# Cross-attention with layer norm on one core: scores of one of four column groups of heads with 128 rows at a time instead of 64

## The chip, the cores and the metric

The kernel runs on one core of a Trainium2 chip. The metric is the device time of one execution in microseconds, median of several executions. An execution profiled by the hardware gives the trace, from which every span and wait below is taken. Engines go by the profile's names: PE is TensorE (PEld its weight loads), DVE is VectorE, ACT is ScalarE, POOL is GpSimd, SP is the engine that issues most transfers.

## The reference

Queries come from `x` (4 batches of 2048 rows, 512 wide), keys and values from a context of 77 rows per batch; 16 heads of 32. After the attention comes the output product, the residual and a layer norm.

```python
qs = (q @ wq).reshape(Bq, Lq, H, HD).transpose(0, 2, 1, 3)
ks_ = (k @ wk).reshape(Bq, Lk, H, HD).transpose(0, 2, 1, 3)
vs = (v @ wv).reshape(Bq, Lk, H, HD).transpose(0, 2, 1, 3)
scores = jnp.einsum('bhqd,bhkd->bhqk', qs, ks_) / jnp.sqrt(jnp.float32(HD))
scores = jnp.where(mask[:, None, :, :], -jnp.inf, scores)
attn_w = jax.nn.softmax(scores, axis=-1)
attn = jnp.einsum('bhqk,bhkd->bhqd', attn_w, vs)
attn = attn.transpose(0, 2, 1, 3).reshape(Bq, Lq, H * HD)
out = attn @ wo + q
mu = jnp.mean(out, axis=-1, keepdims=True)
var = jnp.mean((out - mu) ** 2, axis=-1, keepdims=True)
return (out - mu) / jnp.sqrt(var + EPS) * gamma + beta
```

## The kernel before

**Tiles.** The 8192 rows are 64 tiles of 128 rows. Query projections are made for groups of 512 rows (4 tiles); the product of weights and values goes by pairs of tiles, 256 rows. Products with the 512x512 weights split each operand into a high and a low part and add three products (high by high, high by low, low by high), in 4 steps of the contraction: 12 matmuls with 512 columns for one visit.

**TensorE's work by kind.** Four kinds make up nearly all of it, and each has its letter in the order table:
- Q, line 290 (`q_rows`): one of four 128-column blocks of the query projection of a group of 512 rows, tile `pq`, 12 matmuls, in the shape 128x128 (rows by columns of the array that the weights fill).
- S, line 414 (`scores`): the scores of one tile, in four banks `sc`. Head group `g` (0 to 3) and member `j` (0 to 3) give 16 heads. Heads of one `g` lie on the four 32-row strips of one 128-column block of the projection, so four products with 32 rows of contraction stand side by side in the array. The queries are the weights here; the 77 keys stream. `SR` = 64 splits the tile's 128 query rows into two halves: 4 groups times 2 halves times 4 members are 32 products in the shape 32x64. They are float32, and each is two passes in the profile, two weight loads and two matmul records.
- V, line 507 (`av`): attention weights times values for a pair of tiles, tile `pa`, 16 products in the shape 96x32.
- O, line 579 (`o_proj`): the output product of a tile, `po`, 12 matmuls in the shape 128x128.

**The other engines, per tile.** VectorE takes the scores with the mask and finds the row maxima (line 431, 16 calls), transposes (482), makes the low part of the attention output (540), copies projections (304), adds the residual (588). ScalarE makes the exponentials (446, 16 calls) and some casts; GpSimd normalises (461), splits `x` (273) and applies the affine part (621, 622). Transfers regroup the transposed weights `B` into `PT` (493).

**The order.** The tile framework schedules nothing here. The string `ORDER` lists every step, one word for each: `S36` is the scores of tile 36, `Q38` the third block of group 9, `V15` the values' product of pair 15. The words run in that order on every engine that they use, and semaphores keep the engines apart. Through the middle of the run TensorE's words repeat with a period of two tiles: S, V, S, Q, Q, O, O. Around the change in tile 36 they read S36, V15, S37, Q40, Q41, O31, O30. `SLOTS` names the buffer of every tile in the same order.

**NO_OPs.** `PADS` has one base-36 digit for each visit of kind Q (from the second group on) or O, in the order in which these stand in the program. `pad_steps` spreads that many NO_OPs (line 283, `idle`) over the 11 gaps between the visit's 12 matmuls. Before the change the middle of the run has 20 to 22 in each visit, two in nearly every gap.

Of the kernel before, what the change touches and what calls it, by code (L numbers as in the profile page):

```python
# [17 lines left out]
P = 128  # L18
# [3 lines left out]
NK = 77  # L22
# [11 lines left out]
for b in range(4):  # L34
# [6 lines left out]
SR = 64  # L41
# [128 lines left out]
}  # L170

PADS = (
    "f8680000000000000000000686000cddlmmllllllllmmmmmmmmmmmmmmmmmmmmikkkkkkkkkkkkkkkkkkkkkkkkkkkkkkjkkk00"
    "000000000000000000000000"
)


# [1 line left out]
def xattn_layernorm(  # L179
# [37 lines left out]
    def bank(name):  # L217
        return ps.tile([P, 512], F32, tag="mm" + next(slots["mm"]), name=name)
# [35 lines left out]
    def keys_of(h):  # L254
        return slice(TAIL_K, NK2) if h % 2 == 0 else slice(0, NK)
# [144 lines left out]
    def early_waits(mm, t):  # L400
        after = pe_words[pe_words.index(f"S{t}") + 1]
        for part in parts[int(after[1:])] if after[0] == "V" else ():
            info = mybir.DependencyInfo(mybir.DependencyClass.Sync, mybir.DependencyReason.DATA)
            tc.add_manual_dep(mm.ins, part.ins.name, info, reason="values' product waits ahead of the scores")

    def scores(t):
        qs, first = qd[t // 4], True
        rs = slice((t % 4) * P, (t % 4) * P + P)
        sc = scs[t] = [bank(f"sc_{t}_{j}") for j in range(GH)]
        for g in range(NG):  # L410
            for r0 in range(0, P, SR):
                for j in range(GH):
                    q = slice(HD * j, HD * (j + 1))
                    mm = nc.tensor.matmul(  # L414
                        sc[j][r0 : r0 + SR, g * NK : (g + 1) * NK],
                        qs[q, g, rs.start + r0 : rs.start + r0 + SR],
                        kct[q, g, t // TPB, keys_of(j)],
                        start=True,
                        stop=True,
                    )  # L420
                    if first:
                        early_waits(mm, t)
                    first = False
# [319 lines left out]
    for c in range(0, NC_D, 2):  # L743
# [14 lines left out]
        "i": lambda k, part: cast_xT(k // 2, k % 2 * 2), "j": lambda k, part: split_xT(k // 2, k % 2 * 2),  # L758
        "Q": lambda k, part: q_visit(*divmod(k, 4)), "q": lambda k, part: q_evac(*divmod(k, 4)),
        "S": lambda k, part: scores(k), "T": lambda k, part: maxima(k, q4 * part, q4 * part + q4),  # L760
        "e": lambda k, part: exps(k, q4 * part, q4 * part + q4), "r": lambda k, part: recip(k),
        "n": lambda k, part: normalise(k), "h": recip_half, "m": normalise_half, "t": lambda k, part: transp(k),
# [71 lines left out]
```

## Time and profile before

| what | before |
|---|---|
| median of 3 runs | 510.38 us (510.31 to 512.49) |
| the profiled execution | 509.93 us |
| its span, first to last instruction | 508.1 us |
| granted TensorE clock over the span | 0.998 |
| line 290 (Q), 12 matmuls of one kind each | x256, 395, 383 and 383 ns |
| line 579 (O) | x256, 399, 390 and 390 ns |
| line 507 (V) matmul records | x992, 382 ns |
| line 414 (S) weight loads | x4096, 130 ns |

A record of a matmul covers its whole way through the array, so records of neighbours overlap, and the pace is read from one start to the next. The counts of line 414 are twice those of the products, for the two passes. In rows of a timeline the columns are the start and the length in microseconds, then engine, line, operation, output and inputs, the shape (rows*columns of the array), the size of what streams, and the count.

### The profile page before, as it was taken

To read this page: it belongs to the slowest core of one execution; us is meant where nothing else is said; L and a number is where in the kernel's file an instruction comes from. 1 tells how busy PE (TensorE), PEld (TensorE's weight loads), DVE (VectorE), ACT (ScalarE), POOL (GpSimd) and SP (SyncE) were. 2 spreads that over 40 slices of the span, in tenths; PEclk is the share of its full clock that TensorE was granted. 3 is DMA by queue.
4 is the path that set the end of the run, shared out by engine and by line. 5 is a ranking of instruction groups with operands and counts; after the bars stand their busy time and mean duration, and the time that the engine had idled before them with its cause. 6 is when DMAs were issued, how large, how long until landed. Compare 5 with 4: busy or idle time off the path is not lost.

```text
span 508.1 us, 21810 instructions
## 1 busy us (share of the span) xinstructions
PE 497.6 (98%) x6834; PEld 384.0 (76%) x6834; DVE 471.3 (93%) x2565; ACT 465.6 (92%) x2228; POOL 420.0 (83%) x388
## 2 busy tenths in 40 slices
PE   8999999999999999999999999999999999999994
PEld 6987777777777777777777877777787777776663
DVE  5798999999999999999999999999999999999986
ACT  6699999998999999999999999999999999999622
POOL 2573756999978998989899898888989679999986
PEclk9999999999999999999999999999999999999999
DMA  8947767878987687796877678777777687777755
GB/s 298 397 154 215 177 185 171 239 195 237 261 239 220 192 243 198 204 261 189 237 205 239 198 218 229 213 226 211 225 207 219 182 225 214 209 210 198 213 153 228
DMA packets 59236, 110.96 MB, mean 218 GB/s; under 512 B 9430, under 2 KB 12270, under 8 KB 59126
## 3 DMA queue, kind: packets, MB, share of 16 engines
q1 hardware_dynamic: 54854, 101.63, 69.1%
q0 software_dynamic: 2624, 6.16, 4.4%
q10 hardware_dynamic: 1648, 1.77, 1.4%
q8 instruction: 60, 0.98, 0.9%
q14 instruction: 50, 0.41, 0.3%
HBM read 41.79 MB, written 16.78 MB: 115 GB/s over the span
## 4 chain that ended last, share of the span: by engine, by line
PE 85%; DVE 5%; DMA 4%; POOL 3%; SPq 2%; issue 1%; ACTq 0%; ACT 0%; DVEq 0%
PE pq L290 33%; PE po L579 28%; PE sc L414 10%; PE pa L507 10%; PE pv L341 2%; DVE pbuf L431 1%; DVE B L482 1%; PE pk L313 1%; DMA xtl<-x 1%; DMA PT<-B 1%; SPq L493 1%; DMA first_xth<-xw 1%; POOL mvt L646 1%; PE pq L724 1%; DVE q L304 0%
## 5 line engine op out<-in xcount | busy, mean ns | idle before, releaser
L446 ACT ACTIVATE pbuf<-pbuf,nm 128x77 f32<-128x77 f32 x1024 | 352.4, 350 | 3.6 <-DVE nm L431 3.4
L446 ACT ACTIVATION_READ_ACCUMULATOR pbuf<-pbuf,nm 128x1 f32 x1024 | 195.3, 191 | 0.0
L431 DVE CUSTOM_DVE_ANT_0 pbuf<-sc,mb 128x77 f32<-128x77 f32 x1024 | 170.8, 232 | 6.8 <-PE sc L414 3.6
L461 POOL TENSOR_TENSOR pbuf<-pbuf,ri 128x1232 f32<-128x1232 f32 x63 | 142.8, 2268 | 29.1 <-DVE ri L456 27.6
L579 PE MATMUL po<-woh,AH 128*128 128x512 f32 x256 | 102.1, 399 | 0.4 <-DVE nm L431 0.4
L290 PE MATMUL pq<-xth,wqh 128*128 128x512 f32 (+1 forms) x256 | 101.2, 395 | 0.3
L579 PE MATMUL po<-woh,AL 128*128 128x512 f32 x256 | 99.8, 390 | 0.8 <-DVE AL L540 0.8
L579 PE MATMUL po<-wol,AH 128*128 128x512 f32 x256 | 99.7, 390 | 0.0
L290 PE MATMUL pq<-xth,wql 128*128 128x512 f32 (+1 forms) x256 | 98.1, 383 | 0.0
L290 PE MATMUL pq<-xtl,wqh 128*128 128x512 f32 (+1 forms) x256 | 98.1, 383 | 0.0
L482 DVE STREAM_TRANSPOSE B<-pbuf 128x1280 f32<-128x1280 f32 x64 | 96.1, 1501 | 0.9 <-POOL pbuf L461 0.2
L431 DVE DVE_READ_ACCUMULATOR2_ANT nm<- 128x1 f32 x1024 | 83.8, 82 | 0.0
L273 POOL TENSOR_TENSOR xtl<-xtf,xth 128x1024 fp32r<-128x1024 f32 x28 | 67.3, 2406 | 4.3 <-ACT xth L269 4.3
L622 POOL TENSOR_TENSOR o<-o,bet 128x512 f32<-128x512 f32 x51 | 66.0, 1294 | 4.0
L414 PEld LDWEIGHTS sc<-kct,q 32*64 32x64 f32 x4096 | 51.2, 130 | 22.2 <-issue 11.0
L621 POOL TENSOR_TENSOR o<-o,gam 128x512 f32<-128x512 f32 x51 | 67.0, 1314 | 0.2 <-issue 0.2
L414 PE MATMUL sc<-kct,q 32*64 32x77 f32 x4096 | 60.6, 238 | 0.0
L507 PE MATMUL pa<-PT,vsb 96*32 96x256 f32 x992 | 59.7, 382 | 0.0
L579 PEld LDWEIGHTS po<-woh,AH 128*128 128x128 f32 x256 | 48.0, 188 | 13.9 <-issue 1.7
L290 PEld LDWEIGHTS pq<-xth,wqh 128*128 128x128 f32 x256 | 48.1, 188 | 12.3 <-issue 1.2
L579 PEld LDWEIGHTS po<-woh,AL 128*128 128x128 f32 x256 | 48.1, 188 | 11.6 <-DVE AL L540 1.5
L290 PEld LDWEIGHTS pq<-xth,wql 128*128 128x128 f32 x256 | 48.1, 188 | 9.7
(127 smaller groups left out, 641.9 us busy)
## 6 DMA issues: line engine op xcount, KB each, us to landing
PT<-B SPq DMA_DIRECT2D x337, 128.0 KB
xtf<-xT SPq DMA_DIRECT2D x28, 512.0 KB
o<-x SPq DMA_DIRECT2D x56, 256.0 KB
out<-o SPq DMA_DIRECT2D x56, 256.0 KB
PT<-B POOLq DMA_DIRECT2D x29, 128.0 KB, 3.9
stage_a<-wk SPq DMA_DIRECT2D x4, 256.0 KB
stage_b<-wo SPq DMA_DIRECT2D x4, 256.0 KB
stage_a<-xT SPq DMA_DIRECT2D x2, 512.0 KB
```

The lines of the kernel that those rows point to most:

```text
L273: nc.gpsimd.tensor_tensor(l[:, c : c + 2], fx.pop((g, c)), xh[g][:, c : c + 2].bitcast(F32), ALU.subtract)
L290: nc.tensor.matmul(pq, w[:, c, m * P : (m + 1) * P], r[g][:, c, rs], start=(n == 0), stop=(n == 11))
L341: nc.tensor.matmul(pv[: rows.stop - rows.start], ctx_s[c][i][:, rows], v[c], start=(n == 0), stop=(n == 11))
L414: mm = nc.tensor.matmul(sc[j][r0 : r0 + SR, g * NK : (g + 1) * NK], qs[q, g, rs.start + r0 : rs.start + r0 + SR], kct[q, g, t // TPB, keys ...
L431: nc.vector.tensor_tensor_reduce(pb[:, h // 2, (h % 2) * NK : (h % 2 + 1) * NK], scs[t][j][:, g * NK : (g + 1) * NK], mb[:, t % TPB, keys_ ...
L446: nc.scalar.activation(pb[:, h // 2, (h % 2) * NK : (h % 2 + 1) * NK], pb[:, h // 2, (h % 2) * NK : (h % 2 + 1) * NK], AF.Exp, bias=nmax[t ...
L461: nc.gpsimd.tensor_tensor(pv, pv, rv.to_broadcast((P, NP, 2, NK)), ALU.mult)
L482: nc.vector.transpose(bt.rearrange("p c q r -> p q c r"), pbuf[t % NPB].rearrange("p q (c r) -> p q c r", c=5),)
L507: nc.tensor.matmul(pas[b, g // 2][HD * j : HD * (j + 1), (g % 2) * BLK : (g % 2 + 1) * BLK], vsb[:, 2 * b // TPB, h % 2, HD * (h // 2) : H ...
L579: nc.tensor.matmul(pos[t], a[:, c, rs], w[:, c, :], start=(first and c == 0 and n == 0), stop=(c == NC_D - 1 and n == 2),)
L621: nc.gpsimd.tensor_tensor(o, o, gam, ALU.mult)
L622: nc.gpsimd.tensor_tensor(o, o, bet, ALU.add)
```

## The change

In `scores`, the group `g == 1` takes all 128 rows as weights at once, so that its products have the shape 32x128; the groups 0, 2 and 3 keep their two halves of 64. A tile then has 8 + 4 + 8 + 8 = 28 products. What each bank holds at the end is the same. `PADS` is another string: 1479 NO_OPs in the program instead of 1466, and another distribution. The order of the words, the buffers and the other engines' instructions stay as they were.

```diff
 PADS = (
-    "f8680000000000000000000686000cddlmmllllllllmmmmmmmmmmmmmmmmmmmmikkkkkkkkkkkkkkkkkkkkkkkkkkkkkkjkkk00"
-    "000000000000000000000000"
+    "f8682000000000000000000000000086cddddddb1hllll1dllmmmmmmmmmmmmmmmmmmmmmmmmmmmmmmmmmmmmmkkkkkkkkk4kkkk"
+    "mmmmm0000000000000000000"
 )
...
         for g in range(NG):
-            for r0 in range(0, P, SR):
+            rows = P if g == 1 else SR
+            for r0 in range(0, P, rows):
                 for j in range(GH):
                     q = slice(HD * j, HD * (j + 1))
                     mm = nc.tensor.matmul(
-                        sc[j][r0 : r0 + SR, g * NK : (g + 1) * NK],
-                        qs[q, g, rs.start + r0 : rs.start + r0 + SR],
+                        sc[j][r0 : r0 + rows, g * NK : (g + 1) * NK],
+                        qs[q, g, rs.start + r0 : rs.start + r0 + rows],
                         kct[q, g, t // TPB, keys_of(j)],
```

The first place is TensorE's order in the scores of tile 36. A row is a product: the bank it writes, the keys and queries it reads, and rows by columns of its result. Before, these eight rows are the second column group, its lower and its upper half:

```order
L414 MATMUL sc_36_0_5891<-kct_74,q_9_5475 64x77
L414 MATMUL sc_36_1_5892<-kct_74,q_9_5475 64x77
L414 MATMUL sc_36_2_5893<-kct_74,q_9_5475 64x77
L414 MATMUL sc_36_3_5894<-kct_74,q_9_5475 64x77
L414 MATMUL sc_36_0_5891<-kct_74,q_9_5475 64x77
L414 MATMUL sc_36_1_5892<-kct_74,q_9_5475 64x77
L414 MATMUL sc_36_2_5893<-kct_74,q_9_5475 64x77
L414 MATMUL sc_36_3_5894<-kct_74,q_9_5475 64x77
```

Now the last row of the first group, the four of the second, and the first of the third:

```order
L415 MATMUL sc_36_3_5588<-kct_74,q_9_5169 64x77
L415 MATMUL sc_36_0_5585<-kct_74,q_9_5169 128x77
L415 MATMUL sc_36_1_5586<-kct_74,q_9_5169 128x77
L415 MATMUL sc_36_2_5587<-kct_74,q_9_5169 128x77
L415 MATMUL sc_36_3_5588<-kct_74,q_9_5169 128x77
L415 MATMUL sc_36_0_5585<-kct_74,q_9_5169 64x77
```

Eight products have become four, and the shape changes once ahead of them and once behind.

The second place is TensorE's order in the visit Q30 (third block of group 7), as an example of the NO_OPs that moved. Before, the visit begins so:

```order
L290 MATMUL pq_7_2_4231<-xth_7_3371,wqh_70 128x512
L283 NO_OP x2
L290 MATMUL pq_7_2_4231<-xtl_7_3441,wqh_70 128x512
L283 NO_OP x2
L290 MATMUL pq_7_2_4231<-xth_7_3371,wql_71 128x512
```

And now:

```order
L290 MATMUL pq_7_2_3981<-xth_7_3190,wqh_70 128x512
L283 NO_OP
L290 MATMUL pq_7_2_3981<-xtl_7_3256,wqh_70 128x512
L290 MATMUL pq_7_2_3981<-xth_7_3190,wql_71 128x512
L290 MATMUL pq_7_2_3981<-xth_7_3190,wqh_70 128x512
```

Of 22 NO_OPs in this visit one is left. Elsewhere it goes the other way: the eight visits from Q56 to O48 had none and have 20 to 22.

More of the change, by code (lines that the diff above doesn't have):

```diff
@@ L172 @@
 PADS = (
-    "f8680000000000000000000686000cddlmmllllllllmmmmmmmmmmmmmmmmmmmmikkkkkkkkkkkkkkkkkkkkkkkkkkkkkkjkkk00"
-    "000000000000000000000000"
+    "f8682000000000000000000000000086cddddddb1hllll1dllmmmmmmmmmmmmmmmmmmmmmmmmmmmmmmmmmmmmkkkkkkkkk4kkkk"
+    "mmmmm0000000000000000000"
 )
```

## The prediction

> **What bounds the kernel now.** I read the page first: busy times, granted clock, chain.
>
> ```profile
> span 508.1 us, 21810 instructions
> PE 497.6 (98%) x6834; PEld 384.0 (76%) x6834; DVE 471.3 (93%) x2565; ACT 465.6 (92%) x2228; POOL 420.0 (83%) x388
> PEclk9999999999999999999999999999999999999999
> PE 85%; DVE 5%; DMA 4%; POOL 3%; SPq 2%; issue 1%; ACTq 0%; ACT 0%; DVEq 0%
> L414 PE MATMUL sc<-kct,q 32*64 32x77 f32 x4096 | 60.6, 238 | 0.0
> ```
>
> TensorE is busy all the time, at full clock, and the chain that ended last lies on it for 85%. Four engines are above 80%, though, so I asked next for the stretches between one pair of tiles and the next.
>
> ```profile
> core 0: us, PE busy (x) PEld busy (x) DVE busy (x) ACT busy (x) POOL busy (x), PEclk, DMA share, GB/s
> 264.93:279.68 14.75, 14.75 (x212) 11.46 (x209) 13.54 (x79) 14.40 (x71) 13.47 (x12) 1.00 0.76 225
> 279.68:294.43 14.75, 14.75 (x213) 11.46 (x209) 14.17 (x82) 14.35 (x70) 12.96 (x11) 1.00 0.72 207
> ```
>
> Two tiles take 14.75 us, all of it TensorE. ScalarE has 0.35 us to spare, VectorE 0.6 to 1.2. So a longer score product lengthens the loop at once, while a shorter one may save some 0.3 us a loop before ScalarE holds it. The chain of waits shows the loop's parts:
>
> ```profile
> 109.88 5.68 PE po L579 x24
> 277.00 0.88 PE sc L414 x55
> 277.89 1.86 PE pa L507 x32
> 279.75 0.88 PE sc L414 x53
> 280.63 5.68 PE pq L290 x24
> 286.31 5.44 PE po L579 x24
> ```
>
> A tile's scores take 0.88 us, 64 times. The first row is of two visits without a NO_OP, the last two of visits with 22 each: the visit right behind scores is 5.68 us with and without. NO_OPs are hidden behind matmuls of 0.23 us.
>
> **One tile's scores, record by record.** Each of the 32 products leaves two matmul records and two weight loads (4096 records over 64 tiles). The timeline of tile 36, in windows that end later and later, then its weight loads:
>
> ```profile
> 276.94 0.32 PE L414 MATMUL sc<-kct,q 32*64 32x77 f32 x8
> 276.94 0.39 PE L414 MATMUL sc<-kct,q 32*64 32x77 f32 x16
> 276.94 0.46 PE L414 MATMUL sc<-kct,q 32*64 32x77 f32 x24
> 276.94 0.52 PE L414 MATMUL sc<-kct,q 32*64 32x77 f32 x32
> 277.31 0.51 PE L414 MATMUL sc<-kct,q 32*64 32x77 f32 x27
> 276.94 0.95 PE L414 MATMUL sc<-kct,q 32*64 32x77 f32 x64
> 276.93 0.45 PEld L414 LDWEIGHTS sc<-kct,q 32*64 32x64 f32 x34 [0.35 <-issue]
> L414 PE MATMUL sc<-kct,q x4096: 224/225/277, 20.9 to 466.5; 32*64 32x77 f32 x196
> ```
>
> Eight records run side by side (four row groups of the array times two column halves), and a wave of eight costs 0.067 us (0.39 to 0.46 to 0.52). A record lasts 0.225, so the 32nd starts at 0.52 - 0.225 = 0.295. At the wave pace the 64th would start at 0.295 + 4 x 0.067 = 0.56; it starts at 0.95 - 0.225 = 0.725. So 0.16 us is lost, and the load row tells where: by 277.30 only 34 loads (17 products) have begun, and the next records begin at 277.31. The first 17 products are at hand at once; the other 15 then arrive one per 0.017 us or so ((277.66 - 0.12 - 277.31) / 14, with 0.12 for a product's two passes).
>
> **What a change of shape costs.** The places before and behind:
>
> ```profile
> 276.39 0.39 PE L579 MATMUL po<-wol,AH 128*128 128x512 f32 x1
> 276.62 0.39 PE L579 MATMUL po<-woh,AL 128*128 128x512 f32 x1
> 277.81 0.37 PEld L507 LDWEIGHTS pa<-PT,vsb 96*32 96x32 f32 x12
> 280.56 0.50 PE L290 MATMUL pq<-xth,wqh 128*128 128x512 f32 x1
> 280.90 0.39 PE L290 MATMUL pq<-xtl,wqh 128*128 128x512 f32 x1
> 281.12 0.40 PE L290 MATMUL pq<-xth,wql 128*128 128x512 f32 x1
> 280.67 0.19 PEld L290 LDWEIGHTS pq<-xtl,wqh 128*128 128x128 f32 x1
> ```
>
> Output matmuls follow each other at 0.23, but the scores begin 0.31 behind the last one (276.93 - 276.62): 0.09 more. The last score record starts at 277.66, the values' first load at 277.81: 0.15, where the next wave would have come within 0.067: again 0.09. No load of the new shape was pulled ahead: "[0.35 <-issue]" is a load engine that waits for nothing the profile shows. Then the first 128-column load lies bare: the second matmul comes 0.34 behind the first instead of 0.23, and the second load 0.11 behind the first (280.56, 280.67). So 128 columns load in 0.11 and 64 in about 0.055.
>
> **The change, part by part.** It removes 4 of 32 products a tile: 8 matmul records and 8 loads, 512 of each over the run. It adds two places where the shape changes, 32x64 to 32x128 and back. The trace of before has no change of the column half alone: each of its three kinds of boundary (128x128 or 96x32 against 32x64) changes rows and columns. Upper bound: it costs what these cost. Lower bound: nothing, loads pulled ahead as within the scores. I take the upper one, because all three kinds show the same 0.09 however different their columns are, and no row shows a boundary for less.
>
> Terms per tile, against a score product at the wave pace (0.88 - 0.16 = 0.72):
> - two boundaries. The next wave's first record normally starts 0.067 - 0.047 = 0.02 behind the last record of the one ahead (eight starts 0.0067 apart, estimated from (0.32 - 0.276)/7, with the 0.277 of the source row for the first ones); now 0.15: 2 x 0.13 = +0.26.
> - bare loads: +0.11 into the second group, +0.055 into the third.
> - inside the second group the second pass waits for its 128-column load, 0.11 instead of 0.067: +0.04.
> - four records a wave instead of eight: -0.03.
> - the 0.16 us of late products does not come back: the boundaries give the last 15 more time than they need.
>
> 0.72 + 0.26 + 0.165 + 0.04 - 0.03 = 1.155, so +0.275 per tile. By the skill's page this is what happens: the Trainium skill, TensorEngine Tiling (Array Packing), Key Properties, states that changing the tiling mode, not just the tile, drains TensorE. The three boundaries here agree with 0.09 each; whether it holds for columns alone no run here shows yet, and with no drain the sum would be the first rival's.
>
> The same skill speaks still harder against the change in TensorE: Matmul & The Clock Gate, "What overlaps and what doesn't": loads overlap matmuls in flight only if the row group differs. By that, each pass of the second group would be load plus stream, another 0.067 a tile, and the time 531. The trace disagrees: the load at 280.67 runs while the first matmul on the same rows streams until 280.90.
>
> How many tiles count? The late part of the chain and of the waits:
>
> ```profile
> 402.97 1.20 DVE AL L540 x2
> 415.67 1.42 DVE B L482
> 456.18 1.91 PE pa L507 x32
> 462.30 6.36 DMA xtl<-x
> PEld po L579 <- DVE nm L431: 0.5, 1, 0.5
> ```
>
> Around 402 to 417 VectorE leads and TensorE waits 0.5 us for it (the waits between 411 and 420); a later TensorE uses that up first. Past 458 the chain runs over transfers and VectorE, so the last tile's scores (465.73) do not count. 63 x 0.275 - 0.5 = +16.8. The profiled execution took 509.93 (1.8 around its span): 526.7. The median of the runs shown is 0.45 above it: 527.
>
> **NO_OPs** go from 1466 to 1479 and stand elsewhere (none before, 20 to 22 in eight late visits; 12 to 13 instead of 21 in several early ones). I cost them at nothing: the 5.68 against 5.68 above. They matter as a cover for instruction fetching:
>
> ```profile
> q8 instruction: 60, 0.98, 0.9%
> 203.24 0.96 PE sc L414 x52
> 262.20 0.93 PE sc L414 x55
> ```
>
> 60 packets of 16 KB fit TensorE's some 15,400 instructions, about 256 each (an estimate). Before, a loop's length is nearly a whole number of packets; 32 records fewer a loop shift that, and a late fetch could fall into scores. The worst scores in the loop, whatever their cause, are 0.05 to 0.08 longer than 0.88. The bound is that on every tile, 64 x 0.08 = 5 us; with boundaries inside the scores there is time to spare, so I take 0.
>
> **Rivals.**
> 1. Faster: a change of columns alone drains nothing. Then the 0.16 us pause is what counts. At the wave pace the scores are 0.72; the second group's two loads add 0.04 each, and the first of them starts 0.03 late because both halves must be free: 0.83, or -0.05; the queue allows at most 4 x 0.017 = -0.067. Tiles past 398 hardly count (VectorE leads), say 55 to 60: -2.7 to -4.0, so 506.4 to 507.7, about 507.3. For it: rows stay 32, and loads are pulled ahead freely within the scores. Against: every boundary seen.
> 2. Slower by less: no drain, but the 128-column load must wait until the passes before it have streamed. Rival 1 plus 0.067 on the way in and about 0.05 on the way out: +0.06 a tile, 63 x 0.06 = 3.8, 514. It decides from the point where a load cannot enter a half that still streams.
> 3. No change: rival 1's gain is eaten by ScalarE (0.35 us idle a loop, fully busy in places before 161) or by fetches of 0.05 in most scores: 510 +- 2.
>
> **Numbers.** Forecast (drain) 0.46, its own range 521 to 530; rival 1 0.30, rival 2 0.12, rival 3 0.12. 0.5%, 2.55 us, is about what a measurement of this kernel can tell from no change. Rival 1 is beyond it 4 times in 5: faster 0.24. Same: 0.06 of rival 1 and rival 3, 0.18. Slower: 0.58. The range reaches from rival 1's middle, 506.8, to 530: it leaves out the best of rival 1 and the worst of the drain.
>
> **What would show it.** Right: tile 36's scores at 1.1 to 1.2 us in the chain, gaps of 0.15 before and behind the 32*128 records, 15.3 us a pair, ScalarE idle above 0.8 us a loop. Rival 1: scores at 0.81 to 0.84 with 32*128 loads beginning within 0.03 of the last 32*64 record. Rival 2: about 0.94. I would be wrong in the term of the boundary if the gaps are there but shorter, and in the count of tiles if scores lengthen and the loop does not.

## The result, and the profile after

The changed kernel takes 526.72 us (median of 5 runs, 526.58 to 527.15). The kernel before took 510.59 us beside it (5 runs, 510.31 to 512.49). The ratio is 1.0307, with a 95% interval of 1.0288 to 1.0327: slower by 3%. The profiled execution took 526.61 us.

The page after, the lines that answer to those of before (span, busy times, granted clock, shares of the chain that ended last), and VectorE's reading of the scores:

```profile
span 524.7 us, 20798 instructions
PE 515.4 (98%) x6322; PEld 391.5 (75%) x6322; DVE 473.8 (90%) x2565; ACT 468.5 (89%) x2228; POOL 419.0 (80%) x388
PEclk9999999999999999999999999999999999999999
PE 94%; POOL 3%; DMA 1%; DVE 1%; issue 0%; SPq 0%; ACT 0%; DVEq 0%
L432 DVE CUSTOM_DVE_ANT_0 pbuf<-sc,mb 128x77 f32<-128x77 f32 x1024 | 171.1, 232 | 15.8 <-PE sc L415 12.7
```

TensorE runs 512 matmul records fewer (6322 for 6834) at the same clock and is busy 17.8 us longer. The other engines' busy time has hardly moved, and VectorE waits 12.7 us in all for the scores instead of 3.6 (the row of line 431 before). TensorE leads the chain for 94% of the span instead of 85%: where VectorE and transfers led near the end of before, TensorE does now.

The same stretches from pair to pair as before, busy time of each engine:

```profile
core 0: us, PE busy (x) PEld busy (x) DVE busy (x) ACT busy (x) POOL busy (x), PEclk, DMA share, GB/s
274.00:289.28 15.28, 15.28 (x197) 11.67 (x193) 13.58 (x79) 14.49 (x70) 13.14 (x11) 1.00 0.73 217
289.28:304.57 15.29, 15.29 (x196) 11.68 (x192) 14.14 (x80) 14.50 (x71) 13.30 (x11) 1.00 0.68 202
```

A pair takes 15.28 to 15.29 us instead of 14.75, all of it TensorE. The chain of waits in the loop shows which step grew:

```profile
286.32 1.16 PE sc L415 x56
287.48 1.86 PE pa L508 x32
289.35 1.16 PE sc L415 x56
290.51 5.67 PE pq L290 x24
296.18 5.44 PE po L580 x24
```

Scores went from 0.88 to 1.16 us; values, Q and O are as they were (1.86, 5.67, 5.44). Added up over the run, from each tile's first score record to the first record of the next step, the scores went from 57.4 to 74.3 us, +16.9. All other stretches of TensorE from the first visit of line 290 on together stayed at 425.8 (425.86 and 425.82). The span grew by 16.6, because that first visit begins 0.3 us earlier now (17.92 and 17.60). So the whole lengthening lies in the scores.

Inside tile 36, the timeline in windows that begin and end at different records (start, length, engine, line, operation, shape of the array, what streams, count):

```profile
286.25 0.39 PE L415 MATMUL sc<-kct,q 32*64 32x77 f32 x16
286.57 0.20 PEld L415 LDWEIGHTS sc<-kct,q 32*128 32x128 f32 x4
286.57 0.31 PEld L415 LDWEIGHTS sc<-kct,q 32*128 32x128 f32 x8
286.57 0.46 PE L415 MATMUL sc<-kct,q 32*128 32x77 f32 x8
286.96 0.37 PEld L415 LDWEIGHTS sc<-kct,q 32*64 32x64 f32 x32
287.14 0.34 PE L415 MATMUL sc<-kct,q 32*64 32x77 f32 x16
287.41 0.16 PEld L508 LDWEIGHTS pa<-PT,vsb 96*32 96x32 f32 x8
```

Read them as three changes of shape. The first group's last record ends at 286.25 + 0.39 = 286.64, and the first load of the wide group starts at 286.57. The wide group's last record ends at 286.57 + 0.46 = 287.03, the next narrow load starts at 286.96. The last narrow record ends at 287.14 + 0.34 = 287.48, the values' first load starts at 287.41. Each time the first load of the new shape starts 0.07 us ahead of the modelled end of the last record of the old one, and never earlier, though loads of the same shape are pulled far ahead. The boundaries of before show the same 0.07: the last score record there ends at 277.66 + 0.225, the values' first load starts at 277.81. From record start to load start this is 0.154 us on the way in, behind records of 0.225, and 0.199 on the way out, because the wide group's second-pass records last 0.270 (the 0.045 more is the whole difference). The wide loads of the second pass come 0.11 behind those of the first (0.31 - 0.20). The last 32 loads run through in 0.37 without a gap: the pause of before, between the 17th product and the 18th, is gone.

### The profile page after: what moved, and what is told of

Its sections match the earlier page's. It is cut to its first block, busy times and chain, and to the rows that moved or that the text cites. A ratio compares the mean times of both kernels' runs of the same rounds, so it can differ in the third digit from the quotient of the medians.

```text
span 524.7 us, 20798 instructions
## 1 busy us (share of the span) xinstructions
PE 515.4 (98%) x6322; PEld 391.5 (75%) x6322; DVE 473.8 (90%) x2565; ACT 468.5 (89%) x2228; POOL 419.0 (80%) x388
## 4 chain that ended last, share of the span: by engine, by line
PE 94%; POOL 3%; DMA 1%; DVE 1%; issue 0%; SPq 0%; ACT 0%; DVEq 0%
PE pq L290 33%; PE po L580 31%; PE sc L415 14%; PE pa L508 11%; PE pv L341 2%; PE pk L313 1%; PE pq L725 1%; DMA first_xtl<-xw 1%; POOL mvt L647 1%; PE po L567 1%; POOL PT L494 0%; DMA PT<-B 0%; DVE B L483 0%; POOL xth L623 0%; POOL xtl L622 0%; POOL xth L622 0%
## 5 line engine op out<-in xcount | busy, mean ns | idle before, releaser
L432 DVE CUSTOM_DVE_ANT_0 pbuf<-sc,mb 128x77 f32<-128x77 f32 x1024 | 171.1, 232 | 15.8 <-PE sc L415 12.7
L415 PEld LDWEIGHTS sc<-kct,q 32*64 32x64 f32 (+1 forms) x3584 | 58.6, 138 | 32.8 <-issue 11.8
L415 PE MATMUL sc<-kct,q 32*64 32x77 f32 (+1 forms) x3584 | 78.5, 250 | 0.0
L580 PEld LDWEIGHTS po<-wol,AH 128*128 128x128 f32 x256 | 48.1, 188 | 10.0 <-issue 0.5
```

The source lines that it names most:

```text
L415: mm = nc.tensor.matmul(sc[j][r0 : r0 + rows, g * NK : (g + 1) * NK], qs[q, g, rs.start + r0 : rs.start + r0 + rows], kct[q, g, t // TPB, ...
L432: nc.vector.tensor_tensor_reduce(pb[:, h // 2, (h % 2) * NK : (h % 2 + 1) * NK], scs[t][j][:, g * NK : (g + 1) * NK], mb[:, t % TPB, keys_ ...
L580: nc.tensor.matmul(pos[t], a[:, c, rs], w[:, c, :], start=(first and c == 0 and n == 0), stop=(c == NC_D - 1 and n == 2),)
```

## Experiments: the two parts of the edit, and the place of the wide group

A tile's scores in the tables below reach from the tile's first score record to the first record of the next step, as the median over 64 tiles; the interval is that of the ratio to the kernel before, timed beside it (510.74 us for the first four runs, 509.93 for the next four, 510.44 for the last two).

| run | time, us | ratio, 95% interval | scores of a tile, us |
|---|---|---|---|
| e1_noops_alone | 522.94 | 1.0232 (1.0205 to 1.0260) | 0.882, the second of a loop 1.16 to 3.0 |
| e2_rows_alone | 526.75 | 1.0316 (1.0301 to 1.0332) | 1.162 |
| e3_group0_wide | 525.22 | 1.0287 (1.0268 to 1.0306) | 1.139 |
| e4_group3_wide | 525.39 | 1.0290 (1.0271 to 1.0309) | 1.139 |

**e1_noops_alone** keeps the old scores and takes only the new `PADS`.

```diff
 PADS = (
-    "f8680000000000000000000686000cddlmmllllllllmmmmmmmmmmmmmmmmmmmmikkkkkkkkkkkkkkkkkkkkkkkkkkkkkkjkkk00"
-    "000000000000000000000000"
+    "f8682000000000000000000000000086cddddddb1hllll1dllmmmmmmmmmmmmmmmmmmmmmmmmmmmmmmmmmmmmmkkkkkkkkk4kkkk"
+    "mmmmm0000000000000000000"
 )
```

> The kernel before with only the NO_OP string of the change; all score products stay 32x64. Theory of the boundaries (each change of shape inside the scores empties the array first): the NO_OPs are hidden, so 510.6 +- 1 us, a tile's scores at 0.88 us. Rival, the NO_OPs or where they put the fetches: a good part of the 16 us is here, 514 us or more, with longer visits Q and O or with scores above 0.95 us in many tiles.

It missed: 12 us slower. The chain of waits of e1:

```profile
311.39 0.88 PE sc L414 x53
312.27 1.86 PE pa L507 x32
314.13 0.80 PE sc L414 x49
314.93 0.48 issue
315.41 0.37 PE sc L414 x9
315.77 5.71 PE pq L290 x24
```

The first scores of the loop take 0.88 as ever. In the second ones TensorE stands still for 0.48 us, with nothing in the profile to wait for ("issue"), before the last nine records; in other loops 0.3 to 2 us. The visit Q behind it is 5.71. So the NO_OPs are still hidden where they stand, but they can make something else late. That question gets its own runs below (e9, e10).

**e2_rows_alone** is the other half: the new scores, with the old `PADS`.

```diff
-            for r0 in range(0, P, SR):
+            rows = P if g == 1 else SR
+            for r0 in range(0, P, rows):
```

> The change with the NO_OP string of before: 128 rows in group 1 alone. Theory of the boundaries: the whole loss is here, 526 to 528 us, scores at 1.16 us. Rival, the NO_OPs: clearly below 524 us.

526.75 against 526.72 with both halves of the edit: with these scores the two strings of NO_OPs cost the same, and the shape of the second group makes the whole result. The stalls of e1 are not there: all second scores stand near 1.16.

**e3_group0_wide** and **e4_group3_wide** move the wide group to the first and to the last place, where only one of its two changes of shape lies inside the scores. The old `PADS`, and

```diff
-            rows = P if g == 1 else SR
+            rows = P if g == 0 else SR
```

or `g == 3`.

> 128 rows in group 0 instead of group 1 (NO_OPs of before): one change of shape inside the scores instead of two, and the same four 128-column loads twice. Theory of the boundaries: 0.107 load + passes up to 0.19, boundary 0.20, then three groups at the wave pace: 0.975 us a tile, 63 x 0.095 - 0.5 = +5.5, 516 us. Rival, the wide loads themselves cost the 0.28 us wherever they stand: 1.16 us, 527 us. Rival, a wide load waits only for its own strip of 32 rows: about 0.93 us, 513 us.

> 128 rows in group 3 instead of group 1 (NO_OPs of before): one change of shape inside the scores, behind the late products. Theory of the boundaries: the 24 narrow products end late as before (last one starts its second pass at 0.59), then 0.154 + 0.171 + 0.02 + 0.199: 1.14 us a tile, +15.8, 526 us. So one boundary costs here nearly what two cost in group 1, because the pause of 0.16 us for late products comes back. Rival, wide loads alone: 1.16 us, 527 us (not told apart here, but by group 0). Rival, own strip only: about 0.94 us, 514 us.

e4 came as expected (1.14 and 526). e3 missed by 0.16 us a tile and 9 us in all. The weight loads of e3's tile 36 show why, again in windows that begin at different records:

```profile
285.99 0.31 PEld L415 LDWEIGHTS sc<-kct,q 32*128 32x128 f32 x8 [0.35 <-DMA out<-o]
286.38 0.45 PEld L415 LDWEIGHTS sc<-kct,q 32*64 32x64 f32 x34
286.75 0.29 PEld L415 LDWEIGHTS sc<-kct,q 32*64 32x64 f32 x14
```

Behind the wide group 34 loads, 17 products, run at the wave pace from 286.38; then there is a hole, and the 18th comes at 286.75, 0.375 us behind the first of them. That is the same 17 and the same 0.375 as in the scores of before (loads from 276.93, the next records at 277.31). The pause costs 0.16, and 0.975 + 0.16 = 1.135. I had taken it that a boundary early in the scores gives the later products time to arrive. In e3 it does not: they arrive only 0.375 behind the first product past the boundary, 17 places ahead. One rule fits these runs: no load of a score step starts sooner than 0.375 us behind the load 34 places, or 17 products, ahead of it. In each of the 64 tiles of the kernel before, of e3 and of e4 that is the smallest such distance (0.375 to 0.376). In e3 24 products follow the boundary without a stop, and the limit holds them up. In the change the two boundaries lie between, only 16 products follow the second, and the smallest distance is 0.51: there is no pause.

## Experiments: what the change of shape waits for

Four more, all with the old `PADS`.

| run | time, us | ratio, 95% interval | scores of a tile, us |
|---|---|---|---|
| e5_all_wide | 519.69 | 1.0187 (1.0157 to 1.0216) | 1.061 |
| e6_group1_narrow | 542.14 | 1.0627 (1.0596 to 1.0658) | 1.174, fourteen 1.2 to 3.2 |
| e7_two_members_wide | 533.33 | 1.0454 (1.0424 to 1.0485) | 1.269 |
| e8_groups12_wide | 531.25 | 1.0413 (1.0383 to 1.0444) | 1.253 |

**e5_all_wide** has no change of shape inside the scores: `rows = P` for all four groups. It tells the price of the shape 32x128 from that of changing.

> 128 rows in all four groups (NO_OPs of before): 16 products a tile, eight passes that each wait 0.107 us for a 128-column load, no change of shape inside the scores. Theory of the boundaries: second pass at 0.171, six more at 0.107, stagger 0.02, then 0.199: 1.03 us a tile, +0.15 x 63 - 0.5 = +9, 519.5 us, faster than the change although it has four times as many wide loads. Rival, wide loads cost 0.28 us a group: 0.88 + 4 x 0.28 = 2.0 us, 581 us.

The loads of one tile of e5, up to two points in time:

```profile
285.07 0.20 PEld L415 LDWEIGHTS sc<-kct,q 32*128 32x128 f32 x4 [0.41 <-DVE nm L432]
285.07 0.42 PEld L415 LDWEIGHTS sc<-kct,q 32*128 32x128 f32 x12 [0.41 <-DVE nm L432]
```

Three passes' loads start 0.11 apart ((0.42 - 0.20) / 2), so a wide group of two passes costs 0.22 where a narrow one costs two waves, 0.134: 0.09 more. Four wide groups (1.061) are quicker than one wide among three narrow ones (1.163). The shape itself is the smaller part.

**e8_groups12_wide** puts two wide groups side by side (`rows = P if g in (1, 2) else SR`): one wide group more than the change, and no boundary more.

> 128 rows in groups 1 and 2 (NO_OPs of before): the same two changes of shape as the change, twice the wide loads. Theory of the boundaries: two more passes at 0.107 instead of 0.067: 1.24 us a tile, about 532 us. Rival, wide loads cost 0.28 us a group: 1.44 us, 545 us.

1.253 - 1.163 = 0.09, what e5's pace gives for a wide group in place of a narrow one at the wave pace. So of the 0.44 by which the changed scores stand above 0.72 (1.163 - 0.72), 0.09 belong to the wide group and 0.35 to its two boundaries.

**e7_two_members_wide** asks whether the wide load waits for its own rows of the array or for all of it. In the second group, the members 0 and 1 are done in halves of 64 first, then members 2 and 3 with 128. The rows of members 2 and 3 are last used in group 0.

```diff
-                for j in range(GH):
+            order = [(r0, j, SR) for r0 in range(0, P, SR) for j in range(GH)]
+            if g == 1:
+                order = [(r0, j, SR) for r0 in range(0, P, SR) for j in (0, 1)] + [(0, 2, P), (0, 3, P)]
+            for r0, j, rows in order:
```

> In group 1 members 0 and 1 in halves of 64, then members 2 and 3 with 128 rows (NO_OPs of before): when the wide loads come, the last narrow passes run on strips 0 and 1, the wide loads go to strips 2 and 3. Theory that the whole array is emptied: first group to 0.165, narrow pair to 0.27, then 0.154 + 0.171 + 0.007 + 0.199, and the rest: 1.25 us a tile, longer than the change's 1.16, about 533 us. Rival, a load waits only for what runs on its own strip: nothing to wait for, at most 0.95 us, 514 us. Rival, wide loads cost: half of them, 1.02 us, 519 us.

The timeline of one tile of e7: group 0, all narrow records, and the first wide loads.

```profile
290.40 0.39 PE L417 MATMUL sc<-kct,q 32*64 32x77 f32 x16
290.40 0.51 PE L417 MATMUL sc<-kct,q 32*64 32x77 f32 x24
290.84 0.30 PEld L417 LDWEIGHTS sc<-kct,q 32*128 32x128 f32 x4
```

Group 0 ends at 290.79 and the eight records of members 0 and 1 at 290.91. The wide load of members 2 and 3 starts at 290.84, 0.07 ahead of the end of the other members' records, the same 0.07 as at every boundary; counted from its own rows' last record it would have started at 290.72. So the change of shape waits for the records of the other rows too, and not only for those of its own.

**e6_group1_narrow** changes the shape the other way, to 32x32 (`rows = 32 if g == 1 else SR`, 16 products in that group).

> 32 rows instead of 64 in group 1 (NO_OPs of before): two changes of shape inside the scores, with loads of 32 columns instead of 128, 40 products a tile. Theory of the boundaries: first group to 0.165, boundary 0.154, sixteen tiles side by side until about 0.59 (the late products of the group), boundary 0.154, two groups at the wave pace and the end: 1.2 us a tile, about +20, 530 us. Rival, the cost is that of 128-column loads: it is gone, only eight products more at 0.017 us: 1.01 us, 518.5 us.

A tile takes 1.174, near the 1.2 expected: a change to fewer columns costs about what a change to more does. In the tile that begins at 294.02 the first load of the new shape starts 0.153 us behind the last record's start at both boundaries, 0.154 being the way in of the change. The total missed by 12 us: fourteen scores run 1.2 to 3.2 us. TensorE's weight queue in e6 stood idle before a score with nothing to wait for:

```profile
PEld sc L415 <- issue: 19.5, 42, 1.9
```

and in the kernel before:

```profile
PEld sc L414 <- issue: 11.0, 31, 0.4
```

The longest such stall is 1.9 us instead of 0.4; in e1 it is 1.4. e6 has the old `PADS`, but 32 more TensorE instructions in each scores step, so what follows lies elsewhere in the instruction packets. Whether these are the same stalls as e1's is read from their places in the next section.

## Experiments: NO_OPs and instruction packets

Instructions are fetched in packets, by the prediction's estimate 256 to a packet. From S28 to S35 TensorE has run 170 instructions fewer in e1 than in the kernel before at the same step. So packets end 170 instructions later in the order or, as one packet is like the next, 86 earlier; farther on the 170 shrink to 122. Two runs with narrow scores tell the number of NO_OPs from the place of the ends. **e9_before_shifted** leaves the old string and adds 83 NO_OPs ahead of the loop (35 in Q20, 35 in Q21, 13 in O11), so that the ends lie about where e1 has them. **e10_noops_shifted** takes the new string, which alone made e1, and adds 173 (35 each in O8, Q20, Q21 and O11, 33 in O10). This brings the count from S28 to S35 back to 3 more than in the kernel before, and to 51 more by S46. The first pair of lines is e9 against the kernel before, the second e10 against e1 (e10's expectation names some of the visits otherwise; these are the ones that have them).

```diff
-    "f8680000000000000000000686000cddlmmllllllllmmmmmmmmmmmmmmmmmmmmikkkkkkkkkkkkkkkkkkkkkkkkkkkkkkjkkk00"
+    "f8680000000000000000000686zzdcddlmmllllllllmmmmmmmmmmmmmmmmmmmmikkkkkkkkkkkkkkkkkkkkkkkkkkkkkkjkkk00"
...
-    "f8682000000000000000000000000086cddddddb1hllll1dllmmmmmmmmmmmmmmmmmmmmmmmmmmmmmmmmmmmmkkkkkkkkk4kkkk"
+    "f868200000000000000000000zzzzx86cddddddb1hllll1dllmmmmmmmmmmmmmmmmmmmmmmmmmmmmmmmmmmmmkkkkkkkkk4kkkk"
```

> The kernel before, all products 32x64, with 83 NO_OPs more in three visits ahead of the loops (Q20, Q21, O11: 35, 35, 13); the loops keep their own NO_OPs. Every later packet of 256 TensorE instructions then ends 83 instructions earlier in the loop, about where it ends in the kernel with the change's NO_OP string alone. Theory that the place of the packets' ends in the loop decides: 516 to 525 us, with second scores of a loop above 1.1 us. Rival, the number or the places of the NO_OPs in the loops themselves: 510 to 512 us.

> The kernel before with the change's NO_OP string and 173 NO_OPs more in five visits ahead of the loops (Q17, O9-O8, Q20, Q21, O11 by their order in the string), so that the packets end in the loop where they do in the kernel before; the loops keep the change's NO_OPs. Theory of the packets' ends: most of the 12 us is gone, 510 to 514 us. Rival, the NO_OPs in the loops: 520 us or more, as with the string alone.

| run | time, us | ratio, 95% interval | all 64 scores, us |
|---|---|---|---|
| the kernel before | 510.44 | | 57.4 |
| e1_noops_alone | 522.94 | 1.0232 (1.0205 to 1.0260) | 68.1 |
| e9_before_shifted | 520.16 | 1.0196 (1.0160 to 1.0232) | 64.9 |
| e10_noops_shifted | 512.55 | 1.0037 (1.0021 to 1.0054) | 58.9 |

The old string shifted by 83 loses 9.7 us, in the second scores of the loops (S21 to S37, 1.4 to 1.9 us each). The new string with 173 NO_OPs more, the most of all, is back within 2.1 us of before. So it is not how many NO_OPs there are but where the packets end behind them.

The traces show what the engine lacked. Number TensorE's records in order: matmuls, each with its load, NO_OPs and semaphore instructions. In e1, e6, e9 and e10 there are 34 pauses of more than 0.25 us between two records of one score step, and five of them stand behind its fourth or sixth record. In each of the other 29 (11, 8, 9 and 1) the record behind the pause has the number 192 or 193 within its 256, so that is where packets end, and the 256 holds. And each of the 29 ends 1.2 to 1.6 us after a packet on q8, the queue whose packets the prediction counted, has landed. For the stall of e1 that ends at 315.41, the view of the queues from 312.99 to 313.01 has that packet:

```profile
q8 instruction: 1, 0.02, 292.2%
```

It took 2.922 x 16 x 0.02 = 0.94 us, and landed at 313.94. The stalls of e6 are thus the same as those of e1: TensorE stands at the end of a packet while the next is on its way. The second scores of a loop are hit because there one packet reaches from the first scores over the values into the second, and is used up quickly: in 3.1 us in e1 (280.38 to 283.53), where the packets of the kernel before last 6 to 9 us from 206 to 397. What sets the moment at which a fetch starts stays open; two such packets of e1, which end in S25 and S27, ran through without a stall.

With the wide group in the scores the same shift does no harm (e2 and the change, 526.75 and 526.72). A packet over the same three steps takes 3.9 us there (362.80 to 366.71 in the change). That this longer time is what saves it is likely, and was not tried by itself. The kernel before, the change, e2 to e5, e7 and e8 have no pause of more than 0.25 us inside a score step, so these stalls do not enter the comparisons of their shapes.

## Why the prediction was right

Forecast 527, measured 526.72. By its steps:

- **What bounds the loop.** Right. A longer score step lengthened the pair by twice its growth (2 x 0.28 by the medians; 0.55 from first score record to first score record, 264.93 to 279.68 before and 289.28 to 304.58 now), and nothing else on TensorE moved by more than 0.02. ScalarE's idle time, 15.29 - 14.50 = 0.79 us a loop, is a hair under the "above 0.8" named.
- **The boundary term.** Right, and it carries the result: the step that had no row in the trace of before, that a change of the column half alone costs what the three kinds of boundary there cost. Entry 0.154 for 0.15 forecast; exit 0.199, which was mis-sized by 0.05, since the records that it waits for are longer than narrow ones.
- **Bare loads and the second pass.** The next narrow group's second pass stands 0.05 behind the wave pace as forecast. Between the wide group's first load and its last record's start lie 0.192 us; four starts, a bare load and a second load were forecast at 0.237 (0.11 + 0.107 + 0.02). These 0.045 less cancel the 0.05 more at the exit. That the sum holds so closely, 1.163 for 1.155, is therefore in part luck. (The prediction's (0.32 - 0.276)/7 is 0.0063; the records stand the 0.0067 apart that it used.)
- **The pause that does not come back.** Right, and for the reason given here: the boundaries stretch the smallest distance over 17 products from 0.375 to 0.51. As a rule for any boundary it would be wrong: in e3, where 24 products follow one without a stop, the pause is back.
- **Number of tiles.** 63 x 0.275 - 0.5 = 16.8 for a span that grew by 16.6. The terms are a little otherwise: all 64 tiles count, since TensorE now leads to 498.5, but the mean score before was 0.897 (57.4 / 64), not 0.88, because single scores waited; the mean now is 1.161, so 64 x 0.264 = 16.9, of which the earlier start takes 0.3 back. That the two sums agree to 0.3 us is again in part luck.
- **NO_OPs at nothing.** Right for this kernel (e2), and its bound of 5 us was too low as a general one: with the old scores the same string costs 12 us (e1). The prediction read the cover correctly, matmuls of 0.23 us over each NO_OP, and also named the fetches; it took the worst scores in sight as the bound, and in the kernel before no packet ran out inside the scores. (Seven late visits got 20 to 22 NO_OPs, Q56 to O49, not eight.)
- **The rivals.** That a change of columns drains nothing (507.3) fell with the rows at 286.57 and 286.96. That nothing drains and a wide load only waits until the halves it enters have streamed (514, scores at 0.94) fell with the scores at 1.16, and e7 shows the wait for other rows. No change (510) fell with the result.
- **The range.** The stated 506.8 to 530 holds an unchanged time and even a gain of 3 us, so lying in it says little. What bears the account out is the drain's own 521 to 530, and the rows. (The lower end is called rival 1's middle; 506.4 to 507.7 have theirs at 507.05.)

The Trainium skill, TensorEngine Tiling (Array Packing), Key Properties, says that a change of tiling mode, not of tile, drains TensorE; the trace agrees, now for columns alone: 0.154 and 0.199 us in the change, and the wait for all rows in e7. The reading of TensorE: Matmul & The Clock Gate, "What overlaps and what doesn't", that loads overlap only matmuls of other row groups, would have given 531; the measured 526.72 goes against it, and so do the loads of the second pass in the wide group, which start 0.11 us behind the first while the first pass's records of 0.33 still run on the same rows.

No run was faster than the kernel before: fewer score products never paid, whether with one group of 128 rows, two, or all four (519.69).

## What to carry to other kernels

Keep all small matmuls of a run in one shape of the array: a group that halves its instructions but brings two changes of shape lost 0.35 us a tile at the boundaries (0.28 in all against before, because the pause of 0.16 went and 0.09 came with the wide shape), and even a uniform wider shape lost, since a 128-column load of 0.11 us is longer than the wave of eight narrow records (0.067). Look at how many products run through at once when short matmuls follow long ones (17 here): the pause behind them took 0.16 of the 0.88 us. And compare versions with different instruction counts only after shifting their packets: 83 NO_OPs ahead of the loops took 9.7 us inside them.

## What the runs showed that was not expected

- The load of a new shape starts 0.07 us ahead of the modelled end of the last record of the old one, whichever rows that used, to more columns or to fewer (the change, e7).
- A load of the scores starts no sooner than about 0.375 us behind the one 17 products ahead of it, from the start of the scores (before, e4) as from a boundary that held products up (e3).
- Where TensorE's instruction packets end in a loop is worth 9.7 us in 510 (e9) and 12.2 (e1). 173 NO_OPs ahead of the loops, which bring the ends back near those of before, leave 2.1 (e10). The stalls fall at packet ends and end 1.2 to 1.6 us after a fetched packet has landed (e1, e6, e9, e10).
